# Layer 2 of a four-layer image kernel: taps in two alternating sums of 512, and one gate block moved from VectorE to ScalarE and GpSimd

## The chip, the cores and the metric

The kernel runs on one core of a Trainium2 chip. The metric is device time in microseconds of one whole execution; the median of three runs is given. All data are fp32.

## The reference, cut to what matters

Four layers follow each other on x of shape (2, 64, 256, 256), each as x + layer(groupnorm(x)). The change touches layer 2 alone:

```python
def _L2_conv_ref(x, w_in, w_dw, fft_filter, w_out):
    p = 8
    x = jnp.einsum('bchw,oc->bohw', x, w_in)                  # 64 -> 384 channels
    B, C, H, W = x.shape
    xp = x.reshape(B, C, H // p, p, W // p, p).transpose(0, 1, 2, 4, 3, 5)
    xp = jnp.fft.irfft2(jnp.fft.rfft2(xp) * fft_filter, s=(p, p))   # 8 x 8 patches
    x = xp.transpose(0, 1, 2, 4, 3, 5).reshape(B, C, H, W)
    x = lax.conv_general_dilated(x, w_dw, (1, 1), [(1, 1), (1, 1)], feature_group_count=C)
    x1, x2 = jnp.split(x, 2, axis=1)                          # 192 gates, 192 values
    x = jax.nn.gelu(x1, approximate=False) * x2
    return jnp.einsum('bchw,oc->bohw', x, w_out)              # 192 -> 64 channels
```

## The kernel before

Layer 2 goes over the image in 32 strips of 8 rows. Its front works in units u of 32 columns, eight to a strip: `norm` normalizes (ScalarE), `turn` transposes (TensorE), `fourier` applies the patch transform, `hidden` projects to 384 hidden values per batch (`f`, L915, in PSUM), `scaled` multiplies them by the filter (`gf`, L922, VectorE), `image` transforms back (`pz`, L941), and ScalarE copies the result (L949) into the strip's frames `z`.

The back works on a strip that the front has finished, nine units later. The 384 channels of two batches lie in six blocks of 128 partitions: a0, a1, a2 are gates, b0, b1, b2 values, and each strip has two halves h of four rows. Every block gets the 3 x 3 depthwise convolution, as nine taps. Block a0 does them on TensorE with diagonal matrices (`gate_pe`, `pcv`, L1064) and gets its gelu as it leaves PSUM. The gate blocks named in the line `gps = ...` (L1141) do them as a product on ScalarE (L1017) and an addition on GpSimd (L1021), two rows at a time (`gate_pool`). The rest are on VectorE (`taps_of`): a chain of nine instructions of four rows, 1024 elements, over one PSUM sum `acc` of two banks. These are gate a2 of half 0 (`gate_dve`) and all six value blocks (`value_dve`); each value ends with the multiplication by its gate (L1049). `project` then multiplies by w_out (`po2` in PSUM), and `finish` adds the residual (`xr`, L1111), takes statistics (L1112) and stores two rows.

The order on every engine is written out by hand: under `manual_schedule` each engine runs its instructions in the order of the calls. A unit has two half-steps g; i = 2j + g counts the 16 half-steps of a strip. Each half-step issues `hidden`, some VectorE taps, `scaled`, the remaining taps, perhaps a projection, and then slots n in which an image, one step of `gate_pe` and a share of the `gate_pool` steps follow one another. The shares come from `quota`, so that the lists `dve` and `gps` are spread evenly, `dve` over 16 half-steps and `gps` over the first 14. `flush` issues the gelus of finished `gate_pool` sums. At i = 14 `edges` copies two rows from frame to frame on GpSimd.

[...]f has two buffers (both used by one half-step, one per batch), pz two, pcv one, acc one of two banks, and po2 one that `turn`, `fourier` and `project` share. SBUF holds six `gl` tiles of gated blocks and three `prod` tiles between ScalarE and GpSimd.

Of the kernel before, what the change touches and what calls it, by code (L numbers as in the profile page):

```python
# [13 lines left out]
ALU = mybir.AluOpType  # L14
# [106 lines left out]
class Kernel:  # L121
# [695 lines left out]
    def layer2(self, x, y, coeffs):  # L817
# [16 lines left out]
        with ExitStack() as ctx:  # L834
# [32 lines left out]
            p_f = ctx.enter_context(tc.tile_pool(name="l2pf", bufs=2, space=PSUM))  # L867
            p_z = ctx.enter_context(tc.tile_pool(name="l2pz", bufs=2, space=PSUM))
            p_c = ctx.enter_context(tc.tile_pool(name="l2pc", bufs=1, space=PSUM))
            p_a = ctx.enter_context(tc.tile_pool(name="l2pa", bufs=1, space=PSUM))  # L870
            p_o = ctx.enter_context(tc.tile_pool(name="l2po", bufs=1, space=PSUM))

            x_half, x_T, x_f, gf, z, gl, xres = {}, {}, {}, {}, {}, {}, {}
# [8 lines left out]
                x_half[n] = t  # L882

            def norm(t):
                xn = pool.tile([P, 4, P], F32, name="xn2")
                at = slice(64 * (t % 2), 64 * (t % 2) + 64)
                self.affine(
                    xn.rearrange("p g (i c) -> p i g c", c=16),
                    x_half[t // 2][:, :, at].rearrange("p i (g c) -> p i g c", c=16),
                    coeffs,  # L890
                )
                x_n[t] = xn
# [9 lines left out]
            def fourier(t):  # L902
                pf = p_o.tile([P, 4, P], F32, name="po2")
                for g in range(4):
                    nc.tensor.matmul(pf[:, g], x_T[t][:, g], fwd, start=True, stop=True)  # L905
                xf = pool.tile([P, 4, P], F32, name="xf")
                nc.scalar.copy(xf, pf)
                x_f[t] = xf
# [55 lines left out]
            def near(s, name, m0, r, k):  # L964
                dy, dx = k // 3, k % 3
                p, e = place[name]
                return z[s, p][:, e, m0 + dy : m0 + dy + r, dx : dx + W]

            def taps_of(eng, s, name, m0, r, first, last):

                box = {}

                def step(k):
                    w = taps[name][:, k : k + 1]
                    if k == 0:
                        box["t"] = first()
                        eng.tensor_scalar(box["t"], near(s, name, m0, r, 0), w, None, ALU.mult)  # L977
                        return
                    out = last(box["t"]) if k == 8 else box["t"]
                    eng.scalar_tensor_tensor(  # L980
                        out, near(s, name, m0, r, k), w, box["t"], ALU.mult, ALU.add
                    )

                return [lambda k=k: step(k) for k in range(9)], box

            def new_gl(s, h, i, r):
                t = pool.tile([P, 4, W], F32, name="gl", bufs=6)
                gl[s, h, i] = t
                return t[:, :r]

            def new_acc(r):
                return p_a.tile([P, 4, W], F32, name="acc")[:, :r]

            def gelu(t):
                nc.scalar.activation(t, t, AF.Gelu)
# [31 lines left out]
                        out.append(lambda m=m, k=k: step(m, min(2, r - m), k))  # L1027
                return out

            def gate_dve(s, h, i, r=4):  # L1030
                ops, box = taps_of(
                    nc.vector,
                    s,
                    f"a{i}",
                    4 * h,
                    r,
                    lambda: new_acc(r),
                    lambda t: new_gl(s, h, i, r),
                )
                return ops[:8] + [lambda: (ops[8](), gelu(gl[s, h, i][:, :r]))]  # L1040

            def value_dve(s, h, i, r=4):
                ops, box = taps_of(
                    nc.vector, s, f"b{i}", 4 * h, r, lambda: new_acc(r), lambda t: t
                )

                def gate():
                    t = gl[s, h, i][:, :r]
                    nc.vector.tensor_tensor(t, t, box["t"], ALU.mult)  # L1049

                return ops + [gate]

            def gate_pe(s, h, i, r=4):
                out = []
# [61 lines left out]
            def quota(n, i, parts):  # L1116
                return n * (i + 1) // parts - n * i // parts

            E = mybir.EngineType
            with tc.manual_schedule(engines={E.PE, E.DVE, E.Activation, E.Pool, E.SP}):  # L1120
                frame(0)
                edges(0)
                load_half(0)
                load_half(1)
                norm(0)
                turn(0)
                fourier(0)
                n_u = 8 * nstrip
                dve, pe, gps = [], [], []
                for u in range(n_u + 12):  # L1130
                    t, odd = divmod(u, 2)
                    front = u < n_u
                    v = u - 9
                    s, j = divmod(v, 8)
                    if j == 0 and 0 <= s < nstrip:
                        dve = gate_dve(s, 0, 2)
                        for h in range(2):
                            for i in ((2, 1, 0), (2, 0, 1))[h]:
                                dve += value_dve(s, h, i)
                        pe = gate_pe(s, 0, 0) + gate_pe(s, 1, 0)  # L1140
                        gps = gate_pool(s, 0, 1) + gate_pool(s, 1, 2) + gate_pool(s, 1, 1)  # L1141
                        n_dve, n_gps = len(dve), len(gps)
                    if front:
                        if u % 4 == 2 and u // 4 + 2 < 2 * nstrip:
                            load_half(u // 4 + 2)
                        if not odd and t + 1 < 4 * nstrip:
                            norm(t + 1)
                    if u % 8 == 1 and 0 < u - 1 < n_u:
                        frame(u // 8)

                    out = None
                    if 0 <= v:
                        hv, part = divmod(v - 4, 4)
                        if 0 <= hv < 2 * nstrip and part in (0, 1):
                            reload(*divmod(hv, 2), part)
                        hv, part = divmod(v - 5, 4)
                        if 0 <= hv < 2 * nstrip and part in (0, 1):
                            out = (*divmod(hv, 2), part)
                    for g in range(2):
                        i = 2 * j + g  # L1160
                        left = quota(n_dve, i, 16) if 0 <= v and dve else 0
                        if front:
                            ph = hidden(t, 2 * odd + g)
                        for _ in range(min(2, left)):
                            dve.pop(0)()
                        if front:
                            scaled(t, 2 * odd + g, ph)
                        for _ in range(left - min(2, left)):
                            dve.pop(0)()
                        if out and g == odd:  # L1170
                            po = project(*out)
                        images = ((0, 1), (2,))[g] if 0 < u <= n_u else ()
                        n_pe = min(3, len(pe))
                        for n in range(3):
                            if n < len(images):
                                image(u - 1, images[n])
                            if n < n_pe:
                                pe.pop(0)()
                            if i < 14 and 0 <= v and gps:
                                for _ in range(quota(n_gps, 3 * i + n, 42)):  # L1180
                                    gps.pop(0)()
                            if n == 1 and g == 0 and odd and front and t + 1 < 4 * nstrip:
                                fourier(t + 1)
                        if i == 14:
                            flush()
                            if 0 <= s < nstrip:
                                if s + 1 == nstrip:
                                    frame(nstrip)
                                edges(s + 1)
                        if out and g == 1:  # L1190
                            finish(*out, po)
                        if g == 1 and not odd and front and t + 1 < 4 * nstrip:
                            turn(t + 1)


                assert not (dve or pe or gps)
                s = nstrip
                reload(s, 0, 0)
                for op in gate_pool(s, 0, 1, 1) + gate_pe(s, 0, 0, 1) + gate_dve(s, 0, 2, 1):
                    op()  # L1200
                flush()
                for i in (2, 1, 0):
                    for op in value_dve(s, 0, i, 1):
                        op()
                finish(s, 0, 0, project(s, 0, 0))
# [109 lines left out]
```

## Time and profile before

| | |
|---|---|
| median of three runs | 19662.92 us (19660.62 to 19663.58) |
| the profiled execution: time / span | 19667.66 / 19665.9 us |
| layer 2 in the span | about 15740 to 19340 us |
| busy over the whole span: PE, DVE, ACT, POOL | 14640.5, 18472.7, 11804.0, 16050.1 us |
| busy in 1000 us of layer 2 (17000 to 18000): PE, DVE, ACT, POOL | 884.7, 967.3, 555.0, 580.5 us |

In lines of the profile PE is TensorE's matmuls, PEld its weight loads, DVE VectorE, ACT ScalarE, POOL GpSimd. A group line gives the source line, engine, operation, written and read tiles, shape and count, then busy time in us, mean ns of one, and the engine's idle time just before them with what ended it. A line of waits names who waited for whom, with total us, times and the longest. A timeline line begins with start and length in us. The busy time of TensorE says less than that of the others, since its matmuls overlap.

### The profile page before, as it was taken

What the parts mean: (1) busy time and instruction counts of PE and PEld (TensorE: products, weight loads), DVE (VectorE), ACT (ScalarE), POOL (GpSimd) and SP (SyncE); (2) the same over time, 40 slices, a digit from 0 to 9 for tenths busy, and PEclk for the clock granted to TensorE, in tenths of its full rate; (3) what the DMA queues carried; (4) which work ended last, traced back from release to release, by engine and by line L of the source; (5) the groups of instructions that cost most, each with busy time, mean ns of one, the idle gap of its engine ahead of it and who ended that gap; (6) DMA issues with size and microseconds to landing.
All of it is one profiled execution on the core that took longest, in us unless ns stands there. A gap on an engine that the chain in (4) does not pass through costs nothing. (4 is left out here: it accounts for less than half of the span.)

```text
span 19665.9 us, 162715 instructions
## 1 busy us (share of the span) xinstructions
PE 14640.5 (74%) x48720; PEld 4861.7 (25%) x48720; DVE 18472.7 (94%) x16222; ACT 11804.0 (60%) x16810; POOL 16050.1 (82%) x8070
## 2 busy tenths in 40 slices
PE   7996767776777677767777677676777688888886
PEld 3431111111111111111111111111111154444444
DVE  6888999999999999999999999999999989999997
ACT  2226666666666666666666666666666555555554
POOL 6987888888888888888888888888888855555554
PEclk9996666666666666666666666666666698989898
DMA  3116666666666666666666666666666500000004
GB/s 124 54 50 157 151 151 151 153 149 156 149 154 152 151 151 151 155 147 157 151 153 150 151 152 151 156 148 154 154 150 151 126 28 29 30 30 29 29 27 145
DMA packets 662182, 2438.84 MB, mean 124 GB/s; under 512 B 131888, under 2 KB 201264, under 8 KB 450160
## 3 DMA queue, kind: packets, MB, share of 16 engines
q1 hardware_dynamic: 661296, 2428.43, 51.4%
q8 instruction: 385, 6.31, 0.1%
q14 instruction: 501, 4.10, 0.1%
HBM read 1990.14 MB, written 437.78 MB: 123 GB/s over the span
## 5 line engine op out<-in xcount | busy, mean ns | idle before, releaser
L792 DVE TENSOR_TENSOR_SCAN h<-da,st,h 128x512 f32<-128x512 f32 x8192 | 9838.6, 1263 | 308.2 <-ACT da L789 223.3
L796 POOL TENSOR_TENSOR h<-h,cb 128x2048 f32<-128x2048 f32 x2048 | 9253.1, 4518 | 164.9 <-POOL st L795 0.4
L789 ACT ACTIVATE da<-dl,p_a 128x512 f32<-128x512 f32 x8192 | 5565.3, 688 | 3985.5 <-DVE h L792 3891.2
L561 PE MATMUL py<-h,t_c_quad 128*32 128x512 f32 x16384 | 3253.7, 817 | 1649.1 <-POOL h L796 1648.6
L561 PE MATMUL pb<-bc,t_c_sel 64*128 64x512 f32 x3072 | 2697.0, 972 | 2385.5 <-DVE h L773 2379.9
L773 DVE TENSOR_TENSOR h<-dv,pb 128x2048 f32<-128x2048 f32 x1536 | 3472.3, 2261 | 40.9 <-DMA dv<-d_dv 40.9
L1021 POOL TENSOR_TENSOR gl<-gl,prod 128x512 f32<-128x512 f32 x1544 | 1959.0, 1270 | 1498.7 <-ACT prod L1017 1423.3
L755 POOL TENSOR_TENSOR h<-dv,cb 128x2048 f32<-128x2048 f32 x512 | 2318.7, 4529 | 17.1 <-DMA dl<-d_dl 17.1
L980 DVE SCALAR_TENSOR_TENSOR acc<-z,tap_b,acc 128x1024 f32<-128x1024 f32 (+1 forms) x1560 | 1988.4, 1275 | 38.8
L561 PEld LDWEIGHTS pb<-bc,t_c_sel 64*128 64x128 f32 x3072 | 661.6, 267 | 4411.3 <-DVE h L773 4345.9
L795 POOL COPY st<-h 128x4 f32<-128x4 f32 x2048 | 384.1, 188 | 1365.1 <-DVE h L792 1352.7
L561 PEld LDWEIGHTS py<-h,t_c_quad 128*32 128x32 f32 x16384 | 424.0, 122 | 3815.3 <-POOL h L796 3217.3
L561 PE MATMUL mm<-xin,p_conv 64*128 64x512 f32 x4096 | 1322.9, 775 | 15.2 <-DMA x1t<-y 15.2
L1064 PE MATMUL pcv<-z,diag 128*128 128x512 f32 x2322 | 1174.7, 623 | 19.8 <-ACT gl L1072 16.4
L949 ACT COPY z<-pz 128x512 f32<-128x512 f32 x768 | 456.4, 598 | 1034.1 <-PE pz L941 928.7
L1017 ACT ACTIVATE prod<-z,tap_a 128x512 f32<-128x512 f32 x1544 | 1045.1, 714 | 37.0 <-POOL gl L1021 36.8
L941 PE MATMUL pz<-t_c_inv,gf 128*128 128x128 f32 (+1 forms) x8192 | 1039.4, 309 | 1.9 <-DVE gf L922 1.9
L941 PEld LDWEIGHTS pz<-t_c_inv,gf 128*128 128x128 f32 (+1 forms) x8192 | 849.4, 181 | 520.0 <-issue 311.7
L561 PE MATMUL mm<-u,p_dt 128*128 128x512 f32 x1024 | 931.2, 1064 | 0.0
L561 PE MATMUL py<-u,p_d 128*128 128x512 f32 x1024 | 820.8, 894 | 0.0
L915 PE MATMUL f<-t_w_inT,xf 64*128 64x384 f32 x2048 | 596.7, 616 | 155.9 <-DVE gf L922 154.8
L561 PEld LDWEIGHTS mm<-xin,p_conv 64*128 64x128 f32 x4096 | 460.5, 244 | 982.6 <-issue 982.5
(167 smaller groups left out, 17448.8 us busy)
## 6 DMA issues: line engine op xcount, KB each, us to landing
cb<-d_bc SPq DMA_DIRECT2D x2048, 320.0 KB
dl<-d_dl SPq DMA_DIRECT2D x2048, 256.0 KB
dv<-d_dv SPq DMA_DIRECT2D x2048, 256.0 KB
d_dl<-delta SPq DMA_DIRECT2D x256, 512.0 KB
d_dv<-du SPq DMA_DIRECT2D x256, 512.0 KB
xin<-in_x SPq DMA_DIRECT2D x16, 2048.0 KB
xt<-in_x SPq DMA_DIRECT2D x32, 1024.0 KB
y<-yt SPq DMA_DIRECT2D x128, 256.0 KB
```

What stands on the lines that cost most here:

```text
L561: nc.tensor.matmul(out, lhsT, rhs, start=start, stop=stop)
L755: nc.gpsimd.tensor_tensor(h, t["dv", b], t["cb", b][:, 0].unsqueeze(1).to_broadcast([P, 4, T]), ALU.mult,)
L773: nc.vector.tensor_tensor(h, t["dv", b], pb.unsqueeze(1).to_broadcast([P, 4, T]), ALU.mult)
L789: nc.scalar.activation(da, t["dl", b][:, k], AF.Exp, scale=ws[m]["a"][:, k, j : j + 1])
L792: nc.vector.tensor_tensor_scan(h[:, k], da, h[:, k], state[m, b][:, j, k : k + 1], ALU.mult, ALU.add)
L796: nc.gpsimd.tensor_tensor(h, h, t["cb", b][:, 1 + j].unsqueeze(1).to_broadcast([P, 4, T]), ALU.mult)
L915: nc.tensor.matmul(p, x_f[t][half, g], w_in[half], start=True, stop=True)
L941: nc.tensor.matmul(pz[i * n : (i + 1) * n, k, :, 16 * g : 16 * g + 16], gf[t, 2 * e + g, b][:, c0 : c0 + n], inv, start=True, stop=True,)
L980: eng.scalar_tensor_tensor(out, near(s, name, m0, r, k), w, box["t"], ALU.mult, ALU.add)
L1017: nc.scalar.activation(prod, near(s, name, 4 * h + m, n, k), AF.Copy, scale=w)
L1021: nc.gpsimd.tensor_add(acc, acc, prod)
L1064: nc.tensor.matmul(box["t"], diag[:, k], near(s, f"a{i}", 4 * h + m, n, k), start=k == 0, stop=k == 8,)
```

## The change

VectorE's taps now work on two rows (512 elements) at a time. A block of four rows has two sums, each in a PSUM bank of its own, and the taps go to them in turn: tap 0 of the first, tap 0 of the second, tap 1 of the first, and so on. Gate a2 of half 0 becomes a fourth `gate_pool` block; VectorE begins each strip with the taps of value b2 of half 0, whose sum goes to a `gl` tile, and GpSimd multiplies it by its gate later, at i = 5 (`value_late`). In a half-step four taps (of 512) stand in front of `scaled`, and the remaining ones come after the slots instead of in front of them. In even units `finish` is issued right behind `scaled` of the second half-step, in front of those taps, and no longer at its end; in odd units it stays at the end. A half-step has four slots instead of three. The `gl` tiles become seven, `xn2` has one buffer, `acc` two of one bank. The diff, cut to its core:

```diff
-            p_a = ctx.enter_context(tc.tile_pool(name="l2pa", bufs=1, space=PSUM))
+            p_a = ctx.enter_context(tc.tile_pool(name="l2pa", bufs=2, space=PSUM))
...
-                xn = pool.tile([P, 4, P], F32, name="xn2")
+                xn = pool.tile([P, 4, P], F32, name="xn2", bufs=1)
...
+            def taps_of(s, name, m0, r, last):
+                acc, ops = {}, []
+                def step(k, m, n):
+                    w, src = taps[name][:, k : k + 1], near(s, name, m0 + m, n, k)
                     if k == 0:
+                        acc[m] = p_a.tile([P, 2, W], F32, name="acc")[:, :n]
+                        nc.vector.tensor_scalar(acc[m], src, w, None, ALU.mult)
                         return
+                    out = last(m, n) if k == 8 and last else acc[m]
+                    nc.vector.scalar_tensor_tensor(out, src, w, acc[m], ALU.mult, ALU.add)
+                for k in range(9):
+                    for m in range(0, r, 2):
+                        ops.append(lambda k=k, m=m: step(k, m, min(2, r - m)))
+                return ops, acc
...
-                t = pool.tile([P, 4, W], F32, name="gl", bufs=6)
+                t = pool.tile([P, 4, W], F32, name="gl", bufs=7)
...
+            def value_dve(s, h, i, r=4):
+                ops, acc = taps_of(s, f"b{i}", 4 * h, r, None)
+                def gate(m, n):
+                    t = gl[s, h, i][:, m : m + n]
+                    nc.vector.tensor_tensor(t, t, acc[m], ALU.mult)
+                return ops + [lambda m=m: gate(m, min(2, r - m)) for m in range(0, r, 2)]
+            def value_late(s, h, i):
+                t = pool.tile([P, 4, W], F32, name="gl", bufs=7)
+                ops, _ = taps_of(s, f"b{i}", 4 * h, 4, lambda m, n: t[:, m : m + n])
+                return ops, lambda: nc.gpsimd.tensor_tensor(
+                    gl[s, h, i], gl[s, h, i], t, ALU.mult
                 )
...
-                        dve = gate_dve(s, 0, 2)
-                        for h in range(2):
-                            for i in ((2, 1, 0), (2, 0, 1))[h]:
-                                dve += value_dve(s, h, i)
+                        dve, gate_late = value_late(s, 0, 2)
+                        for h, i in ((0, 0), (0, 1), (1, 0), (1, 2), (1, 1)):
+                            dve += value_dve(s, h, i)
                         pe = gate_pe(s, 0, 0) + gate_pe(s, 1, 0)
-                        gps = gate_pool(s, 0, 1) + gate_pool(s, 1, 2) + gate_pool(s, 1, 1)
+                        gps = []
+                        for h, i in ((0, 2), (0, 1), (1, 2), (1, 1)):
+                            gps += gate_pool(s, h, i)
...
-                        for _ in range(min(2, left)):
+                        soon = min(4, left)
+                        for _ in range(soon):
                             dve.pop(0)()
                         if front:
                             scaled(t, 2 * odd + g, ph)
-                        for _ in range(left - min(2, left)):
-                            dve.pop(0)()
+                        if out and g == 1 and not odd:
+                            finish(*out, po)
                         if out and g == odd:
                             po = project(*out)
                         images = ((0, 1), (2,))[g] if 0 < u <= n_u else ()
-                        n_pe = min(3, len(pe))
-                        for n in range(3):
+                        n_pe = min(4, len(pe))
+                        if i == 5 and 0 <= s < nstrip:
+                            gate_late()
+                        for n in range(4):
...
-                                for _ in range(quota(n_gps, 3 * i + n, 42)):
+                                for _ in range(quota(n_gps, 4 * i + n, 56)):
                                     gps.pop(0)()
...
+                        for _ in range(left - soon):
+                            dve.pop(0)()
...
-                        if out and g == 1:
+                        if out and g == 1 and odd:
                             finish(*out, po)
```

More of the change, by code (lines that the diff above doesn't have):

```diff
@@ L967, in near @@
                 return z[s, p][:, e, m0 + dy : m0 + dy + r, dx : dx + W]
[L969 to L974, printed above, removed]
+            def taps_of(s, name, m0, r, last):
+                acc, ops = {}, []
+                def step(k, m, n):
+                    w, src = taps[name][:, k : k + 1], near(s, name, m0 + m, n, k)
                     if k == 0:
-                        box["t"] = first()
-                        eng.tensor_scalar(box["t"], near(s, name, m0, r, 0), w, None, ALU.mult)
+                        acc[m] = p_a.tile([P, 2, W], F32, name="acc")[:, :n]
+                        nc.vector.tensor_scalar(acc[m], src, w, None, ALU.mult)
                         return
[L979 to L984, printed above, removed]
+                    out = last(m, n) if k == 8 and last else acc[m]
[4 more added lines that the diff above has]
+                return ops, acc
             def new_gl(s, h, i, r):
-                t = pool.tile([P, 4, W], F32, name="gl", bufs=6)
+                t = pool.tile([P, 4, W], F32, name="gl", bufs=7)
                 gl[s, h, i] = t
                 return t[:, :r]
-            def new_acc(r):
-                return p_a.tile([P, 4, W], F32, name="acc")[:, :r]
             def gelu(t):
@@ L1028, in gate_pool, with gate_dve @@
                 return out
[L1030 to L1038, printed above, removed]
-                )
[L1040 to L1051, printed above, removed]
+            def gate_dve(s, h, i, r):
+                t = new_gl(s, h, i, r)
+                ops, _ = taps_of(s, f"a{i}", 4 * h, r, lambda m, n: t[:, m : m + n])
+                return ops + [lambda: gelu(t)]
+            def value_dve(s, h, i, r=4):
[9 more added lines that the diff above has]
+                    gl[s, h, i], gl[s, h, i], t, ALU.mult
+                )
             def gate_pe(s, h, i, r=4):
```

## The prediction

> **What bounds the kernel now.** Layer 2 is the stretch from about 15,740 to 19,340 us, 31 strips of 8 rows that overlap with the front (projection, filter) and a last one without it. The busy time of a stretch inside it was read first; the columns are length, then PE, PEld, DVE, ACT and POOL busy, granted clock, DMA share, GB/s:
>
> ```profile
> 17000.00:18000.00 1000.00, 884.70 (x4198) 485.56 (x4196) 967.27 (x988) 555.01 (x911) 580.45 (x488) 0.90 0.09 29
> ```
>
> VectorE is full (967 of 1000), TensorE is at 885, ScalarE and GpSimd have over 40% free, DMA nothing to do. The groups by line and form, from 15,800 to 19,340, say of what:
>
> ```profile
> L980 DVE SCALAR_TENSOR_TENSOR acc<-z,tap_b,acc 128x1024 f32<-128x1024 f32 x1536 | 1976.7, 1287 | 37.8
> L1021 POOL TENSOR_TENSOR gl<-gl,prod 128x512 f32<-128x512 f32 x1536 | 1953.2, 1273 | 1498.1 <-ACT prod L1017 1423.3
> ...
> L1017 ACT ACTIVATE prod<-z,tap_a 128x512 f32<-128x512 f32 x1536 | 1041.2, 715 | 33.5 <-POOL gl L1021 33.3
> ...
> L922 DVE TENSOR_TENSOR gf<-feff,f 128x384 f32<-128x384 f32 x990 | 501.0, 547 | 37.3 <-PE f L915 37.3
> ```
>
> The taps are the bulk of VectorE. The waits (16,000 to 19,300) show who limits whom:
>
> ```profile
> POOL gl L1021 <- ACT prod L1017: 1275.8, 529, 13.2
> ...
> PE po L897 <- DVE xr L1111: 217.5, 57, 4.5
> ...
> DVE gf L922 <- PE f L915: 33.1, 29, 2.3
> ```
>
> VectorE waits for f about once per strip, some 1.1 us; TensorE waits for xr twice per strip, 3.8 us each. The timeline of VectorE shows what dependence costs:
>
> ```profile
> 17062.19 5.26 DVE L980 SCALAR_TENSOR_TENSOR acc<-z,tap_b,acc 128x1024 f32<-128x1024 f32 x4
> 17067.35 1.01 DVE L922 TENSOR_TENSOR gf<-feff,f 128x384 f32<-128x384 f32 x2
> 17068.28 2.61 DVE L980 SCALAR_TENSOR_TENSOR acc<-z,tap_b,acc 128x1024 f32<-128x1024 f32 x2
> ```
>
> Four taps in 5.26 us, each of 1.29: they start 1.325 apart, 35 ns after the one before has ended. The gf that follows, which needs none of them, starts 0.09 before the last tap ends, so that tap held the engine for 1.197. Likewise the second gf starts 0.465 after the first, of 0.547. Last, the timeline of TensorE from the start of a strip (VectorE starts it at 17119.93):
>
> ```profile
> 17115.57 2.11 PE L915 MATMUL f<-t_w_inT,xf 64*128 64x384 f32 x4 [1.13 <-DVE gf L922]
> 17117.60 2.27 PE L941 MATMUL pz<-t_c_inv,gf 128*128 128x128 f32 x12
> ...
> 17126.38 0.92 PE L915 MATMUL f<-t_w_inT,xf 64*128 64x384 f32 x4
> ...
> 17130.89 0.92 PE L915 MATMUL f<-t_w_inT,xf 64*128 64x384 f32 x4
> ...
> 17138.83 0.92 PE L915 MATMUL f<-t_w_inT,xf 64*128 64x384 f32 x4
> ```
>
> From f to f is one half-step g (16 per strip). In the first, f takes 2.11 instead of 0.92 and twelve pz 2.27 instead of about 1.2: TensorE runs at half speed after its slack at the strip's end.
>
> [...]
>
> **The change part by part, per strip.**
>
> VectorE before: 63 taps (45 followed by a dependent one, 45 x 1.325 = 59.6; 18 by something else, 18 x 1.197 = 21.5), 6 gates (7.6), 32 gf x 0.465 = 14.9, four xr and stats (0.714 + 0.611) = 5.3, small gaps 0.5: 109.4, with the wait for f 110.2. The first gf of a strip is at 17122.45 and eight strips on at 18004.03: 110.2.
>
> *Offload.* Block a2 leaves VectorE: 9 taps, and the late product b2 x a2 (1.2) goes to GpSimd: some 13 us less.
>
> *Two sums of 512.* 54 taps become 108, of which none needs the one just before it. Not in the trace: a tap of 512 behind another tap. [...]so a pair costs 1.326, as one dependent tap does now; against the 18 that already ran free this loses 2 us. Lower bound 0.60: the independent 512-wide products of layer 0 (L366, L371) start 0.597 apart. Upper bound 0.79: no overlap at all, 0.755 (the 256-wide taps take 487 ns, 1.046 ns per further element) and 35 ns. I take 0.663[...].
>
> VectorE after: 108 x 0.663 = 71.6, ten half gates of 0.605 = 6.1 (1.138 less 512 elements), 14.9, 5.3: **97.8**, 6.11 per half-step.
>
> *GpSimd and ScalarE.* 16 adds more, at 1.356 from start to start (1.272 and 80 ns); 64 make 86.8. The product of 1024 by 256 and 512 wide adds (0.728, 1.272): 2.36. Edges 3.5. Sum 92.6 against 68.6 now. ScalarE: 18 activations more at 0.619, 11 us onto some 58. Both fit inside 97.8; GpSimd barely.
>
> *TensorE.* Each half-step now takes four diag matmuls (pcv) instead of three, so 36 are done in nine half-steps, not twelve. From f to f without waits, the first nine took 10.8, 4.5, 7.9, 4.95, 7.0, 6.4, 6.1, 4.95, 7.0 = 59.6 (fourth and fifth from equal half-steps without a wait); a fourth pcv adds 0.89 each, 67.6. f has two PSUM buffers, both used by one half-step, so f(0) starts when gf of the last half-step has read them, 3.2 us into it: 2.9 before the strip starts. f(9) then starts at 64.7 and is ready at 65.6. VectorE wants it after nine half-steps and four taps: 9 x 6.11 + 2.65 = 57.6. **It waits 8.0 us**, spread over the odd half-steps. Afterwards TensorE has 2 to 5 us of work per half-step and is early again, but VectorE has nothing with which to catch up. Behind a late gf stand all the taps of that half-step, and behind these the gates.
>
> *xr and stats in front of the taps* (even steps): turn (L897) no longer waits the 3.8 us; without that, nine half-steps would be later still. It is counted above. The store of y is issued some microseconds earlier on SP, whose queue is nearly empty here; no DMA is added.
>
> *Buffers.* One xn2 for two: turn of the last tile is two half-steps past when norm writes. Seven gl for seven blocks: each is reused a strip later. PSUM stays at eight banks (acc 1 x 2 banks, then 2 x 1). These cost nothing.
>
> Sum: 97.8 + 8.0 = 105.8 against 110.2, 4.4 x 31 strips = 136. The last strip has no front: before 95 us (19211.8 to 19306.8); after, GpSimd's 93 or so sets it, 2 less. Total 138. The profiled execution took 19667.66 around its span of 19665.9; less 138 it would be 19530. The median of the runs is 4.7 lower: **19525**.
>
> **Rivals.**
>
> *VectorE alone sets the pace* (TensorE keeps full speed through the strip's end, or half-steps are shorter than summed): for it, only the first half-step is slow; against it, the slack at the end grows. Without the slow start (10.8 against 7.0 for the like half-step later on: 3.8) 102.0, 8.2 x 31 + 2 less: 19405; with no wait at all 97.8, 19280.
>
> *Shorter taps*, 0.60: VectorE alone would need 91.0 (97.8 less 108 x 0.063), 5.69 per half-step, and want f(9) at 53.6; it comes at 65.6 as before, so 12.0 of waiting and 103.0: 7.2 x 31 + 2 less, 19440.
>
> *ScalarE and GpSimd couple the engines.* Prods have three buffers; where GpSimd is behind, ScalarE waits and with it the copies of pz and the gelu that frees pcv. Four us more per strip eat the gain: 19600 to 19690.
>
> *Slower: GpSimd becomes the bound.* It has 92.6 us of work and now waits 43 us a strip for prods (1275.8 over 30 strips), 12 of them at the strip's start. These waits come mostly from the order in which prods are handed out and shrink as it fills; beyond 17.6 us of them the strip is longer than 110.2. At 21 it is 113.6: 3.4 x 31, 19770. Against it: the first add comes about 6 us into the strip, so the last ends near 98, and the edges near 102. That taps do not overlap after all (0.79) also ends here: 108 x 0.127 more, 111.5, 1.3 x 31, 19705; near 0.77 the gain is gone.
>
> **How the numbers follow.** TensorE's nine half-steps as summed, 19460 to 19590: 0.58. Better (first two rivals below 19460): 0.16. Coupling, 19590 to 19700: 0.14. Slower: 0.12. 0.2% is 39 us, about what a measurement of this kernel can tell from no change, so faster begins below 19624: 0.58 + 0.16 and a quarter of the coupling, 0.77; same 0.10; slower 0.13. The range, 19400 to 19650, leaves out the case of no wait, the far end of coupling and the slower ones.
>
> **What would show it.** In the profile after: taps of 512 that take 0.755 and start 0.663 apart; gf waiting for f, some 250 us in total against 37, in the odd half-steps up to the ninth; turn no longer waiting for xr; adds at 2050 of 1273 ns; strips 105.8 apart. Taps at 0.79, strips over 110, or GpSimd without gaps while VectorE waits for its gelu would make it wrong.

## The result, and the profile after

| | before | after |
|---|---|---|
| median | 19663.25 us (19660.62 to 19664.69, 6 runs) | 19522.56 us (19520.90 to 19524.39, 6 runs) |
| profiled execution: time / span | 19667.66 / 19665.9 us | 19522.79 / 19521.0 us |
| mean strip with front | 110.2 us | 105.78 us |

The changed kernel takes 0.9929 of the time, with a 95% interval of 0.9916 to 0.9941: 141 us less. The prediction said 19525 and 105.8 per strip. A strip is measured from the first `gf` of one to the first `gf` of the next, over some 28 strips in the middle of layer 2.

The same stretch of the changed kernel as was shown of before (length, then PE, PEld, DVE, ACT, POOL busy, clock, DMA share, GB/s):

```profile
17000.00:18000.00 1000.00, 899.82 (x4399) 500.43 (x4396) 922.51 (x1496) 694.89 (x1141) 827.36 (x675) 0.93 0.10 31
```

VectorE has fallen from 967 to 923 of 1000, so it is no longer full; ScalarE and GpSimd took what it gave away. Its groups by line and form, from 15,800 to 19,200:

```profile
L1020 POOL TENSOR_TENSOR gl<-gl,prod 128x512 f32<-128x512 f32 x2048 | 2600.9, 1273 | 658.0 <-ACT prod L1016 545.2
L981 DVE SCALAR_TENSOR_TENSOR acc<-z,tap_b,acc 128x512 f32<-128x512 f32 x3008 | 2035.0, 748 | 0.0
...
L922 DVE TENSOR_TENSOR gf<-feff,f 128x384 f32<-128x384 f32 x988 | 499.7, 546 | 171.7 <-PE f L915 171.7
...
L1039 DVE TENSOR_TENSOR gl<-gl,acc 128x512 f32<-128x512 f32 x320 | 212.3, 680 | 92.5 <-ACT gl L994 79.9 <-ACT gl L1070 12.6
...
L1047 POOL TENSOR_TENSOR gl<-gl 128x1024 f32<-128x1024 f32 x32 | 75.9, 2370 | 0.0
```

The taps never wait (0.0 idle), but two others do: `gf` for f, 172 us where it was 37, and `gl`, the half gate, for a gelu. The waits from 16,000 to 19,160 give the same from the side of who is waited for:

```profile
POOL gl L1020 <- ACT prod L1016: 444.0, 389, 9.3
...
ACT gl L994 <- POOL gl L1020: 230.1, 153, 4.2
...
DVE gf L922 <- PE f L915: 157.5, 100, 2.4
...
PE po L897 <- DVE xr L1109: 132.3, 28, 4.7
...
DVE gl L1039 <- ACT gl L994: 75.0, 30, 7.2
...
PE pcv L1062 <- ACT gl L1070: 37.1, 32, 5.2
```

GpSimd's waiting fell from 1276 to 444 us; `turn` (L897) waits for xr once per strip (28 times) and not twice (57), but 4.7 us each time where it was 3.8. ScalarE's gelu L994 waits 230 us for GpSimd's last addition, where the same gelu (L995) waited 58 before; that VectorE's gate waits behind it is new. VectorE's timeline at half-steps 6 and 7 of one strip shows how the taps stand, and a wait for f:

```profile
17108.79 2.71 DVE L981 SCALAR_TENSOR_TENSOR acc<-z,tap_b,acc 128x512 f32<-128x512 f32 x4
17111.41 1.01 DVE L922 TENSOR_TENSOR gf<-feff,f 128x384 f32<-128x384 f32 x2
17112.34 4.70 DVE L981 SCALAR_TENSOR_TENSOR acc<-z,tap_b,acc 128x512 f32<-128x512 f32 x7
17119.29 1.02 DVE L922 TENSOR_TENSOR gf<-feff,f 128x384 f32<-128x384 f32 x2 [2.25 <-PE f L915]
```

Seven taps of 0.748 take 4.70: (4.70 - 0.748) / 6 = 0.66 from start to start, each 0.09 before its predecessor's end. Then 2.25 us of nothing, since f is late. Counted by half-step over 28 strips, VectorE waits for f 0.77, 1.59, 0.88 and 2.25 us in half-steps 1, 3, 5 and 7, sum 5.5; 2.3 for the gelu L994 in half-step 7, where it gates (0,1); and 0.4 for pcv's gelu L1070. Together **8.2 us per strip**; 105.78 less 8.2 leaves 97.6 of its own work.

That sum was predicted, but it doesn't say why the wait is there: because TensorE has that much to do, because ScalarE and GpSimd are coupled, or because of something else. The experiments are about that.

### The profile page after: what moved, and what is told of

Its sections match the earlier page's. It is cut to its first block, busy times and chain, and to the rows that moved or that the text cites. A ratio compares the mean times of both kernels' runs of the same rounds, so it can differ in the third digit from the quotient of the medians.

```text
span 19521.0 us, 166010 instructions
## 1 busy us (share of the span) xinstructions
PE 14578.1 (75%) x48720; PEld 4850.7 (25%) x48720; DVE 18176.5 (93%) x17790; ACT 12176.5 (62%) x17418; POOL 16771.1 (86%) x8614
## 5 line engine op out<-in xcount | busy, mean ns | idle before, releaser
L1020 POOL TENSOR_TENSOR gl<-gl,prod 128x512 f32<-128x512 f32 x2056 | 2606.7, 1271 | 658.5 <-ACT prod L1016 545.2
L981 DVE SCALAR_TENSOR_TENSOR acc<-z,tap_b,acc 128x512 f32<-128x512 f32 (+1 forms) x3032 | 2046.7, 746 | 1.0
L1016 ACT ACTIVATE prod<-z,tap_a 128x512 f32<-128x512 f32 x2056 | 1410.4, 715 | 194.8 <-POOL gl L1020 190.5
L922 DVE TENSOR_TENSOR gf<-feff,f 128x384 f32<-128x384 f32 x1024 | 518.1, 547 | 218.7 <-PE f L915 218.7
```

What stands on the lines that cost most here:

```text
L922: nc.vector.tensor_tensor(o, feff, ph[b], ALU.mult)
L981: nc.vector.scalar_tensor_tensor(out, src, w, acc[m], ALU.mult, ALU.add)
L1016: nc.scalar.activation(prod, near(s, name, 4 * h + m, n, k), AF.Copy, scale=w)
L1020: nc.gpsimd.tensor_add(acc, acc, prod)
```

## The experiments

Each was timed beside the kernel before, whose median was 19662 to 19665 us every time. "Strip" and VectorE's waits per strip are counted as above.

| run | median us | ratio to before, interval | strip us | for f | for gelu L994 | for pcv's gelu |
|---|---|---|---|---|---|---|
| the change | 19522.56 | 0.9929 [0.9916, 0.9941] | 105.78 | 5.5 | 2.3 | 0.4 |
| x1_alt_only | 19689.57 | 1.0012 [1.0006, 1.0019] | 111.0 | 0.7 | 0 | 0 |
| x2_offload_only | 19529.24 | 0.9931 [0.9916, 0.9945] | 105.7 | 6.1 | 2.4 | 1.2 |
| x5_finish_end | 19524.48 | 0.9928 [0.9913, 0.9943] | 105.8 | 5.5 | 2.3 | 0.4 |
| x3_fewer_pcv | 19470.79 | 0.9901 [0.9885, 0.9918] | 104.1 | 4.6 | 2.0 | 0 |
| x4_pool_order | 19506.91 | 0.9921 [0.9907, 0.9936] | 105.4 | 7.4 | 0 | 0.4 |
| x6_pace | 19540.38 | 0.9942 [0.9925, 0.9958] | 105.8 | 1.5 | 4.7 | 2.1 |
| x7_both | 19527.53 | 0.9932 [0.9917, 0.9947] | 105.8 | 4.1 | 0 | 4.1 |
| x8_flush4 | 19508.08 | 0.9922 [0.9907, 0.9936] | 105.4 | 3.8 | 0 | 3.9 |
| x9_spread | 19529.66 | 0.9933 [0.9916, 0.9949] | 105.8 | 0.5 | 0.5 | 7.4 |
| x11_late_only | 19497.06 | 0.9916 [0.9899, 0.9932] | 105.0 | 6.0 | 1.5 | 0 |
| **x10_late_spread** | **19261.40** | **0.9795 [0.9781, 0.9810]** | **97.3** | 0 | 0 | 0 |
| x12_flush2 | 19329.29 | 0.9832 [0.9817, 0.9847] | 99.4 | 0.1 | 0 | 2.0 |

### Which part brings the time: x1 and x2

x1 keeps the two sums and leaves gate a2 on VectorE, with the value blocks in the order of before:

```diff
-                        dve, gate_late = value_late(s, 0, 2)
-                        for h, i in ((0, 0), (0, 1), (1, 0), (1, 2), (1, 1)):
-                            dve += value_dve(s, h, i)
+                        dve = gate_dve(s, 0, 2, 4)
+                        for h in range(2):
+                            for i in ((2, 1, 0), (2, 0, 1))[h]:
+                                dve += value_dve(s, h, i)
...
-                        for h, i in ((0, 2), (0, 1), (1, 2), (1, 1)):
+                        for h, i in ((0, 1), (1, 2), (1, 1)):
...
-                            gate_late()
```

> The taps take turns in sums of 512, but gate a2 of half 0 stays on VectorE. Theory (the turns give nothing, the moved block gives all): 126 taps x 0.658 + 12 half gates x 0.598 + gf 14.9 + xr and stats 5.3 = 110.3 us of VectorE per strip, and about 1 us of waiting for f, since nine half-steps of TensorE (67.6) fit nearly into nine of VectorE (62): 111 per strip, 0 to 40 us slower than the kernel before, 19660 to 19705. Rival (the turns themselves save the 35 + 92 ns of every dependent tap): 45 x 0.127 = 6 us per strip less than before, 19480.

x2 makes the opposite cut, the offload with one sum of 1024:

```diff
-            p_a = ctx.enter_context(tc.tile_pool(name="l2pa", bufs=2, space=PSUM))
+            p_a = ctx.enter_context(tc.tile_pool(name="l2pa", bufs=1, space=PSUM))
...
-                    for m in range(0, r, 2):
-                        ops.append(lambda k=k, m=m: step(k, m, min(2, r - m)))
+                    for m in range(0, r, 4):
+                        ops.append(lambda k=k, m=m: step(k, m, min(4, r - m)))
...
-                        soon = min(4, left)
+                        soon = min(2, left)
```

> The block is moved and everything else is as in the changed kernel, but each VectorE tap has 1024 elements again and depends on the one before. Theory: VectorE's own work is the same within 2 us per strip (54 taps of 1.325 or 1.197 against 108 of 0.658), and TensorE's nine half-steps are unchanged, so the strip is again near 106 us: 19500 to 19560. Rival (the turns were needed for the gain): VectorE 6 us per strip longer, about 19700.

x1 takes 19690, 0.1% more than before; its strip is 0.8 us longer. x2 takes 19529, and its interval covers that of the change. So the offload brings all of the gain, and the alternation nothing. A pair of taps of 512 takes 2 x 0.658 = 1.316 us, where a tap of 1024 took 1.325 with a dependent one behind it and 1.197 without: against the tap with no dependent one behind it the two halves cost 0.119 us more (1.316 less 1.197), and that is nearly as much as the gap behind a dependent tap had cost (1.325 less 1.197, or 0.128). For VectorE the alternation is even a small loss. x2's waits sum to 9.7 us, so its own work is 105.7 less 9.7, or 96.0 us per strip, against 97.6 in the change; the waiting hides these 1.6 us (the gates, which are halved too, included).

### The stores' place: x5

`finish` goes back to the end of the half-step in even units too.

```diff
-                        if out and g == 1 and not odd:
-                            finish(*out, po)
...
-                        if out and g == 1 and odd:
+                        if out and g == 1:
```

> The sum with the projection goes back to the end of the half-step in even units too. As predicted (turn waits 3.8 us again in the fourth half-step, and f after it is later by as much): 3 to 4 us per strip more, 19620 to 19650. Rival (VectorE is itself held by f in that half-step, and the shorter one ends before TensorE reaches turn): under 1 us per strip, 19510 to 19550.

19524 against 19523, as the rival had it, and VectorE has the same waits in the same half-steps. Of x5's waits from 16,000 to 19,160:

```profile
PE po L897 <- DVE xr L1109: 187.6, 28, 6.7
```

`turn` waits once per strip here too, in half-step 11, 6.7 us instead of 4.7. The other wait of the kernel before, in half-step 3, stays away although `finish` is back at its old place. The longer wait costs nothing: moving `finish` was no part of the gain.

### Is it TensorE's amount of work: x3

Four of the nine pcv matmuls of each half block are left out, so TensorE has 16 of 36 less per strip.

```diff
+                        if k not in (3, 4, 5, 6):
                             nc.tensor.matmul(
```

> Leaves out four of the nine diagonal matmuls of block a0 (k = 3 to 6), all else in its place. Theory (TensorE's nine half-steps make VectorE late): they shrink by 16 x 0.89 = 14 us to 53, below VectorE's 55, so the waits of gf for f (5.6 us per strip) go; the gate's wait for its gelu (2.5) may stay or grow: 98 to 101 us per strip, 19290 to 19370. Rival (GpSimd with ScalarE is what spaces the strips): no gain from less TensorE work, within 30 us of 19522.

A pcv step takes 0.89 us (in the trace of before three take 2.67, from 17128.22 to the next f at 17130.89). With 16 x 0.89 = 14 us less for TensorE in each strip, the strip became only 1.7 us shorter, and VectorE still waits for f 4.6 us. The 19471 us lie outside the theory's range and outside the rival's. The waits (16,000 to 19,160) name another brake:

```profile
ACT gl L994 <- POOL gl L1020: 234.9, 183, 4.2
...
PE pcv L1063 <- ACT gl L1071: 181.9, 61, 10.2
...
DVE gf L922 <- PE f L915: 131.7, 69, 4.0
```

TensorE now waits 6 us per strip (181.9 over some 30) for the gelu that empties the single pcv buffer; in the changed kernel that was 37.1 us in all. After this wait it is slow as well: in half-step 7 f takes 1.49 us, the mean of 28 strips, where the changed kernel has 0.92. In ScalarE's fixed order a gelu that waits for GpSimd (L994) stands ahead of the one for pcv; that this makes the latter late is argued here, and x12 will show it for another order. So x3 doesn't settle the question: leaving work out made TensorE wait elsewhere, and the time saved didn't reach f.

### Taking the waits away one by one: x4, x6, x7, x8

x4 lets GpSimd make gate (0,1), which VectorE needs first, ahead of (0,2), and moves the late product to i = 8:

```diff
-                        for h, i in ((0, 2), (0, 1), (1, 2), (1, 1)):
+                        for h, i in ((0, 1), (0, 2), (1, 2), (1, 1)):
...
-                        if i == 5 and 0 <= s < nstrip:
+                        if i == 8 and 0 <= s < nstrip:
```

> GpSimd adds up gate a1 of half 0 before a2, and multiplies the late product at i = 8 instead of 5, so the gelu of a1 is there when VectorE's gate asks for it. Theory (in the eighth half-step two waits lie over each other: VectorE for that gelu, 2.3 us, and behind it for f of the tenth, which is only 0.4 us earlier): the gate's wait goes, f's comes in its place, 0.4 to 1.6 us per strip gained: 19470 to 19510. Rival (the waits add up): 2.3 us per strip, 19450.

x6 thins out the pcv matmuls after half-step 4:

```diff
-                        n_pe = min(4, len(pe))
+                        n_pe = min(4 if i < 5 else 3, len(pe))
```

> Three diag matmuls per half-step instead of four from the sixth half-step on, so TensorE has up to 3.6 us less by the tenth; GpSimd's order as in the changed kernel. Theory (two waits over each other): f comes earlier, but the gate's gelu is timed by GpSimd, so VectorE waits for it longer: 0 to 1.3 us per strip gained, 19480 to 19525. Rival (TensorE alone): the waits for f in the eighth half-step go, 2.3 us, 19450.

x7 makes both edits, and x8 moves the gelu of GpSimd's sums two steps back besides, so that ScalarE doesn't stand before GpSimd's last addition:

```diff
-                    if k == 2:
+                    if k == 4:
                         flush()
```

> Both edits of the two kernels above. Theory: only together do they free VectorE: 3 to 4.5 us per strip, 19380 to 19430, more than the sum of the two alone. Rival (independent waits): the sum of the two gains.

> As the kernel with both edits, and the gelu of a finished GpSimd sum is issued two taps later (k = 4 instead of 2), when its last addition is surely done. Theory (ScalarE stands some 7.7 us per strip in front of that gelu until GpSimd is done, and behind it stand the copies of pz and the gelu that frees pcv, so TensorE and f wait): ScalarE's wait for GpSimd at the gelu goes nearly to 0, and 0.5 to 2 us per strip more are gained, 19330 to 19410. Rival (ScalarE has slack enough): within 10 us of the kernel with both edits.

x4, x6 and x8 each removed the wait that they were aimed at, or most of it (in x8 ScalarE's for GpSimd at L994 fell from x7's 208.5 to 46.0 us, 16,000 to 18,900). But x4 and x8 got no more than 16 us of the 250 or so that VectorE's waits make in 31 strips, and x6 and x7 were not faster than the change at all. Only x4 came out in its theory's range; x6, x7 and x8 are slower than theirs, and x8, 19 us faster than x7, fits its rival as little. In x4 the gelu L994 went from 2.3 to 0 and f from 5.5 to 7.4. In x6 f went from 5.5 to 1.5, L994 from 2.3 to 4.7 and pcv's gelu from 0.4 to 2.1. In x7 L994 is gone, f is 4.1 and pcv's gelu 4.1. In all of them the sum is 7.7 to 8.3. The theory that x4 and x6 would pay together fell with x7. A sum that stays the same whichever wait is taken from it suggests that all of them are one delay, seen at different places.

### One deadline, and two edits that only work together: x10, x11, x9

Nearly half of the waiting in x7 and x8 falls in half-step 10, where VectorE gates (1,0), the second block whose gate TensorE makes. By then TensorE must have done all 36 pcv matmuls and the front of ten half-steps, in VectorE's 10.3 x 6.1 us; in the five half-steps left it has a front with no pcv, and can't work ahead, since f has two buffers and VectorE must read them first. If this is the cause, the gate of (1,0) has to come later, and pcv has to use the time that this gives.

x10 builds on x8. The second half of value (1,0) goes to an SBUF tile, and its gate becomes VectorE's last instruction of the strip; pcv is spread over 14 half-steps; (0,1) is gated ahead of (0,0), so that pcv's first block also has longer.

```diff
+            def value_own(s, h, i):
+                own = pool.tile([P, 2, W], F32, name="own", bufs=1)
+                ops, acc = taps_of(s, f"b{i}", 4 * h, 4, lambda m, n: own if m else acc[m])
+                def gate(m, v):
+                    t = gl[s, h, i][:, m : m + 2]
+                    nc.vector.tensor_tensor(t, t, v, ALU.mult)
+                return ops + [lambda: gate(0, acc[0])], [lambda: gate(2, own)]
...
-                t = pool.tile([P, 2, W], F32, name="xr", bufs=3)
+                t = pool.tile([P, 2, W], F32, name="xr", bufs=2)
...
-                        for h, i in ((0, 0), (0, 1), (1, 0), (1, 2), (1, 1)):
-                            dve += value_dve(s, h, i)
+                        own, gate_own = value_own(s, 1, 0)
+                        for h, i in ((0, 1), (0, 0), (1, 0), (1, 2), (1, 1)):
+                            dve += own if (h, i) == (1, 0) else value_dve(s, h, i)
+                        dve += gate_own
...
-                        n_pe = min(4 if i < 5 else 3, len(pe))
+                        n_pe = min((2, 3, 3, 3, 2, 3, 3, 3, 2, 3, 2, 3, 2, 2)[min(i, 13)], len(pe))
```

> The run with the flush two steps later, and in it: the second half of VectorE's value (1,0) goes to an SBUF tile of its own and meets its gate only as VectorE's last instruction of the strip, not in half-step 10; so the 36 pcv matmuls need not be done by then, and are spread over half-steps 0 to 13 (2 or 3 each). xr gets two buffers instead of three to make room. Theory (TensorE must squeeze 36 pcv and ten half-steps of front work in ahead of one gate, and only moving that gate frees VectorE): waits for f fall to 1 to 2 us a strip, pcv's gelu under 1, strip 98 to 101 us, 19300 to 19400 in all. Rival (the wait is kept by ScalarE's and GpSimd's chain, which has some 93 to 98 us a strip itself): another wait takes their place, strip within 1 us of 105.4, 19475 to 19540.

x11 is x10 with `n_pe = min(4, len(pe))`, the late gate alone:

> The same late gate of (1,0), but pcv keeps four matmuls per half-step in the first nine. Theory: VectorE's wait for f comes from four pcv per half-step, so the late gate alone brings little: f waits 5 to 8 us a strip, strip 104 to 106, 19480 to 19530. If the gate's deadline alone were the matter, it would be as fast as the run with the spread matmuls.

x9 is x8 with the new order of (0,1) and (0,0) and the matmuls spread as far as the old gate lets them, `n_pe = min((2, 4, 2, 4, 2, 4, 3, 4, 3, 4, 4)[min(i, 10)], len(pe))`:

> The other half of the fastest run so far (late gate and spread matmuls, 19261): VectorE gates (1,0) in half-step 10 as in the run with the flush two steps later, and the 36 pcv matmuls are spread as far as that gate lets them, in the order 2,4,2,4,2,4,3,4,3,4,4, ended in half-step 10. To let the first half-steps have fewer, VectorE takes (0,1) ahead of (0,0). Theory (the gate's deadline is what makes TensorE late): the wait stays, for pcv's gelu in half-step 10 and for f, 5 to 8 us a strip, strip 103 to 106, 19440 to 19530. Rival (a better spread alone is enough, and the late gate only happened to be with it): strip below 100, under 19350.

x10 takes 19261, 261 us or 1.3% less than the change and less than its theory had; x11 takes 19497 and x9 19530, each in its theory's range. Beside x8, on which all three build, the late gate alone (x11) is 11 us faster and the spread alone (x9) 22 us slower; together they are 247 us faster. The two spreads are not the same, since the old gate makes x9's end in half-step 10. The same 1000 us of x10:

```profile
17000.00:18000.00 1000.00, 927.53 (x4776) 501.53 (x4776) 998.59 (x1626) 751.37 (x1236) 895.48 (x730) 0.99 0.11 34
```

and two of its groups by line and form, 15,800 to 18,900:

```profile
L922 DVE TENSOR_TENSOR gf<-feff,f 128x384 f32<-128x384 f32 x990 | 499.3, 544 | 4.7 <-PE f L915 4.7
...
L1039 DVE TENSOR_TENSOR gl<-gl,acc 128x512 f32<-128x512 f32 x254 | 162.2, 678 | 1.7 <-ACT gl L994 1.7
```

VectorE is busy 998.6 of 1000 and waits for next to nothing. The strip is 97.3 us, where the prediction had 97.8 for VectorE alone. In the two halves the delay sits in one place each. x11's waits and x9's (VectorE's own, 16,000 to 18,900), first x11:

```profile
DVE gf L922 <- PE f L915: 166.3, 95, 2.4
DVE gl L1039 <- ACT gl L994: 42.0, 28, 1.5
```

then x9:

```profile
DVE gl L1039 <- ACT gl L1070: 198.9, 27, 7.5
DVE gl L1039 <- ACT gl L994: 14.8, 15, 1.5
DVE gf L922 <- PE f L915: 13.5, 22, 0.7
```

With four pcv in each of nine half-steps it is f that comes late (x11). With fewer at first, f is in time, and the whole delay stands before the gate in half-step 10 (x9), once per strip, as its timeline shows:

```profile
17131.16 1.01 DVE L922 TENSOR_TENSOR gf<-feff,f 128x384 f32<-128x384 f32 x2
17139.43 0.69 DVE L1039 TENSOR_TENSOR gl<-gl,acc 128x512 f32<-128x512 f32 x1 [7.26 <-ACT gl L1070]
```

How late f comes follows from the number of pcv matmuls ahead of it. From f(0) to f(9) TensorE takes 67.0 us in the change, with 36 of them in between, 63.3 in x8 with 32, 59.8 in x9 with 28 and 57.0 in x10 with 24 (means of 28 strips). Here are these two f in one strip of x10, 56.6 us apart:

```profile
17065.41 1.38 PE L915 MATMUL f<-t_w_inT,xf 64*128 64x384 f32 x4 [1.73 <-DVE gf L922]
...
17122.03 0.92 PE L915 MATMUL f<-t_w_inT,xf 64*128 64x384 f32 x4
```

So two limits lie over each other, and each alone is enough to keep the wait. If all 36 pcv stand in the first nine half-steps, f is late; if some are moved behind f, the gate in half-step 10 waits for them. The cause is the deadline that this gate sets for pcv: only a later gate lets the matmuls be spread, and only the spread makes use of the later gate.

One rival has to be weighed. In x10, where pcv also stand in TensorE's slack at the strip's end, TensorE runs less at half speed too: its granted clock is 0.99 of full speed in these 1000 us, against 0.93 in the change. The traces bound what this is worth. In the strips in which TensorE is soonest back at full speed the change takes 104.0 us, x9 104.5, x11 103.4 and x10 97.1. So slow starts make less than 2 of the 8.2 us.

### What is left of the coupling: x12

x12 is x10 with the gelu of GpSimd's sums back at k = 2.

> The fastest run with one line back: finished sums of GpSimd get their gelu at step k = 2 of the next one, not at k = 4, so ScalarE meets the gelu sooner and waits there for GpSimd (some 8 us a strip in the changed kernel, 1.6 in the fastest run). Theory (this wait only hurt because pcv was on a deadline): no difference that can be told, strip 97 to 98, 19245 to 19280. Rival (ScalarE standing still holds up pz and pcv by itself): VectorE waits again, strip 99 to 102, 19310 to 19410.

19329, 68 us more: the theory expected no difference, and the rival was right. The waits, 16,000 to 18,900:

```profile
ACT gl L994 <- POOL gl L1020: 280.1, 204, 2.4
...
DVE gl L1057 <- ACT gl L1080: 56.3, 29, 2.8
```

In x10 the first of these is 48.4 us. ScalarE standing before GpSimd delays the gelu of pcv (L1080), and with it the first half gate of (1,0), by 2.0 us a strip. Between x7 and x8 the same edit was worth 0.1% and no more; there the deadline lay over it.

## Why the prediction was right, point by point

**The taps.** The estimate was 0.755 long and 0.663 apart; measured are 0.748 and 0.658. The 0.663 was the author's estimate; the trace of before gives 0.662: a tap of 1024 held VectorE for 1.197 us with nothing dependent behind it, and from a tap of 256 to one of 1024 (487 and 1290 ns, the medians) an element costs 1.046 ns, so 512 fewer cost 0.535 us less. The alternation was put at a loss of 2 us of VectorE's time; x2 beside the change gives 1.6, the halved gates included: right in sign, a little smaller.

**The offload.** Predicted 97.8 for VectorE's own work; 97.6 remain when the waits are subtracted, and x10 runs at 97.3. The late product took 2.37 us (predicted 2.36), and there are 2048 additions of 1273 ns (predicted about 2050). GpSimd, at 827 of 1000, didn't become the bound.

**TensorE's nine half-steps.** Predicted 67.6 from f(0) to f(9), and a start at half speed in every strip. The timeline of TensorE in the changed kernel, the f of two successive strips' first half-steps, and f(9) of the second:

```profile
16959.24 2.11 PE L915 MATMUL f<-t_w_inT,xf 64*128 64x384 f32 x4 [0.57 <-DVE gf L922]
...
16971.05 0.92 PE L915 MATMUL f<-t_w_inT,xf 64*128 64x384 f32 x4
...
17066.79 1.37 PE L915 MATMUL f<-t_w_inT,xf 64*128 64x384 f32 x4 [0.57 <-DVE gf L922]
...
17075.08 0.92 PE L915 MATMUL f<-t_w_inT,xf 64*128 64x384 f32 x4
...
17131.98 0.92 PE L915 MATMUL f<-t_w_inT,xf 64*128 64x384 f32 x4
```

The first half-step takes 11.8 us in one strip and 8.3 in the next. TensorE's granted clock is 0.50 from 16953.70 to 16966 in the first of them and 1.00 from 16968.4 to 16980; in the second it is 0.50 from 17061.25 to 17066 and 1.00 from 17066.5 to 17100. f(9) comes 65.2 us after f(0) in the quick strip, and 3.5 more in the slow one; the mean of 28 strips is 67.0, for the 67.6. That is why most strips alternate, about 107.5 and 104.0. So the sum was right, though of its start at half speed only every second strip has the whole.

**The wait, 8.0 us.** The sum is right: 8.2. Its parts are not: 5.5 for f, where all 8.0 were to be, and 2.7 for gelus. f's waits end in half-step 7, not 9, since VectorE loses 2.3 us there to the gelu of (0,1) and f catches up in that time. The 250 us of gf waiting for f came to 172. The rival "ScalarE and GpSimd couple the engines" was thus at work inside the sum, without adding to it: x4 takes its wait away, and f's grows from 5.5 to 7.4, now with 1.9 in half-step 9. That the sum held although a part of it was unforeseen is therefore hardly luck: TensorE's lateness was the limit, and the gelu's wait only lay over it.

**The wrong step** is `finish`: `turn` was to wait no longer for xr, and "without that, nine half-steps would be later still". It still waits, 4.7 us per strip; and x5 undoes the edit, and nothing is later. Of the two waits before, the one within the nine half-steps (in half-step 3) is gone with or without the edit. The edit acts on the other, in half-step 11, where TensorE has slack: with the shorter wait for xr (4.7 us for 6.7) its wait for VectorE to free f in half-step 14 is longer (3.7 for 1.9).

**What the prediction didn't see** is why TensorE is late. Its sum, f ready at 65.6 and wanted at 57.6, was right, but it took the 36 pcv in the first nine half-steps as given. x10 shows that the same work fits once some of it is due later, and x9 that the gate in half-step 10 is what forbids this. The margin was in the order of VectorE's list, not in TensorE's speed. x10's 19261 us are about what the first rival had put for no wait at all, 19280.

**The ends of layer 2.** From the first gf to the last the strips gave 131 us, and the stretch behind the last gf 9 more: 140, for the 138 predicted as 136 and 2. That the whole came within 3 us of the median is luck in this: one part was 5 too high and the other 7 too low.

## What to carry to other kernels

Take the engine times per stage, then ask for each consumer by when its producer's work is due: an engine that fits in the mean can still be late if most of its work is due before two thirds of the stage are over. If one wait after another is removed and their sum stays the same, stop removing waits and look for the deadline behind them; moving it and spreading the work may each do nothing alone, as here, so try both together. Splitting a dependent chain in two pays only where the gap between dependent instructions is larger than what the split adds to an instruction without that gap; here it was 0.128 us (1.325 less 1.197) against 0.119 (1.316 less 1.197), and the taps that had no such gap made it a loss. In x10, where VectorE is the limit, the one sum of 1024 might therefore be faster by up to x2's 1.6 us per strip; no run tried it.

## What the runs showed of the hardware that was not expected

The late half gate of x10 reads two SBUF tiles (L1057, `gl<-gl,own`). In 18 of 32 executions it took 679 to 684 ns, like its neighbour that reads a PSUM sum (median 677); in others up to 1402. x10's timeline of VectorE and GpSimd, one of the longest:

```profile
18233.49 1.04 POOL L957 COPY z<-z 128x1032 f32<-128x1032 f32 x1
18233.64 1.27 DVE L1039 TENSOR_TENSOR gl<-gl,acc 128x512 f32<-128x512 f32 x2
...
18234.65 1.04 POOL L957 COPY z<-z 128x1032 f32<-128x1032 f32 x1
18234.84 1.40 DVE L1057 TENSOR_TENSOR gl<-gl,own 128x512 f32<-128x512 f32 x1
```

The copy of `edges` began 0.19 us before the gate and ended at 18235.69; the gate ended 0.55 later, so that most of its usual 0.68 came after the copy. It is so in all 13 executions that took over 700 ns: such a copy was under way when the gate began, and the gate ended 0.54 to 0.55 us after it. In the 18 of usual length none was, or only in its last 0.1 us. A copy that began during a gate took 1.33 to 1.49 us instead of 1.04. In the timeline above, the two gates ahead of the late one, with one operand in PSUM, ran beside another such copy at their usual length. The group's mean is 842 ns, so the later ends cost x10 about 0.16 us a strip (842 less 683).

The alternation of slow and quick strips is described above, but not settled. The slack at the end of the strip before is alike (3.67 and 3.54 us of waiting in one piece), and behind it f takes 2.11 us in both (from 16953.70 and from 17061.25). But the granted clock goes from 0.50 to 1.00 at 16967.3 in the one, 13.6 us after that f began, and at 17066.3 in the other, 5.1 us after. What decides this the runs don't show.
